# Cross-attention and an RWKV block in one kernel: the mixes behind the second norm, and the mean of the first, are emitted further behind what they read

## The chip, the cores and the metric

The kernel runs on one core of a Trainium2 chip. The metric is the device time of one execution in microseconds (us); less is better. Five engines of the core run their own instruction streams: TensorE (PE) multiplies matrices, VectorE (DVE), ScalarE (ACT) and GpSimd (POOL) do elementwise work, and SyncE (SP) issues DMA transfers. Each engine takes its instructions strictly in the order of the program; an instruction that waits for another engine holds up everything behind it on its own engine.

## The reference

`reference` chains two layers over 16 batches of 112 tokens with 512 features.

1. Cross-attention: layer norm of a context of 375 rows per batch, keys and values from it, queries from x, 16 heads of 32, softmax, output projection, and `x + tanh(gate) * out`.
2. An RWKV block: a first layer norm (`ln1`), token-shift mixes, a small tanh network that makes five mixed inputs, projections to r, k, v, gate and decay w; the recurrence

```
a = k_t[..., :, None] * v_t[..., None, :]
out = jnp.einsum('bhi,bhij->bhj', r_t, u * a + s)
s = a + w_t[..., :, None] * s
```

   over the tokens; a group norm, gate and output projection `x1 = x + og * g @ Wo.T`; a second layer norm `xc = _ln(x1, ln2_w, ln2_b)`; two mixes `xk2 = xc + sx2 * ffn_maa_k` and `xr2 = xc + sx2 * ffn_maa_r` with the token before; and `x1 + sigmoid(xr2 @ Wfr.T) * (relu(xk2 @ Wfk.T)**2 @ Wfv.T)`.

All values are float32.

## The kernel before, in words

Features lie on partitions (4 chunks of 128, called c), tokens on the free axis. Two batches make a group of N = 224 tokens; there are NG = 8 groups. Four parts are Python generators that emit instructions and yield a cost after each step:

- `attention()` runs over all 16 batches and, for each, over four sets of four heads. Names: `pa`, `pk`, `pv` (transposed context, keys L234, values L245 and their products in PSUM), `kT` (keys copied out by ScalarE, L240), `ps` (scores, L298), `pr` (scores plus mask, by VectorE, L309; exponentials in place, by ScalarE, L318), `pt`/`prT` (transposed, L329 to L338), `po`/`oR` (attention outputs and their copy by ScalarE, L353), `pp` (output projection).
- `front(g)`: first layer norm of group g (`ln1`), the difference to the token before (`sx`), the mix `mx` (L534), the tanh network (`pth`, `th`), and the five mixed inputs `xm` (`pxm`, `pxm_b`, L558, L564).
- `middle(g)`: projections `pv`, `pk`, `pr`, `pw` (L180, L684), then 16 steps n of the recurrence: keys times values `kv` (values spread over partitions by DMA, L718; products on VectorE and GpSimd, L731; the first column L739 or L741), the scan on VectorE (`st`, L754), its product with r on GpSimd (L758), and a sum on TensorE (`acc`, L770). It also emits the group norm and gate of the first half of the features (`gm`, `gv`, `gsq`).
- `back(g)`: group norm of the other half, `po1` (L180 again), the second layer norm (`ln2`, tiles `xc`, `sq2`), the two mixes `xk` and `xr` (L853 on ScalarE, L857 on VectorE), and the feed-forward products `pfk`, `pfr`, `pfv`.

The layer norm is one helper for both norms. GpSimd adds the four chunks pairwise (`halves`, L482 and L483), TensorE multiplies the sum with a constant matrix for the mean (L488), VectorE subtracts it (L496), ScalarE squares (L497) and loads its table for logarithm and exponential (L466), GpSimd adds the squares, TensorE makes the variance (L488), ScalarE makes the inverse deviation in two steps (L470, L471), and VectorE multiplies it in, in two halves (L506). For the last group's first norm and the last two groups' second norm (`late`) TensorE sums all four chunks itself. Between these steps stand the yields 2.5, 1, 4 and 1.

The order of emission is a loop at the end. Each part has a place on a common scale on which attention takes 92 cost units for one group; the part with the smallest place emits its next step, and its place grows by the step's cost times a rate. The rate of a part is its length divided by its sum of costs, `FRONT = (0.35, 38.0)`, `MIDDLE = (0.75, 119.0)`, `BACK = (0.8, 65.0)`; the last but one group has a shorter front and middle (`AHEAD_OF_LAST`). So a cost that is added in one step moves the steps behind it, against those of the other parts.

Emission is not yet the order on an engine: a scheduler of the framework places the instructions of each engine by its own estimates. What stands under `tc.high_priority(AHEAD)` goes ahead of what was emitted shortly before it; the mixes L853 and L857 and the relu L868 don't stand under it, most copies out of PSUM do.

PSUM has two pools that matter here. `ps_mm` has 2 buffers, used in turn by everything that TensorE makes for one copy (`pa`, `pk`, `pv`, `po`, `mean`, `var`, `pw`, `pfk` and so on): a tile can be begun when the copy of the tile two before it is done. `ps_s` has 4 buffers for `ps`, `pt` and `pxm`. Weights come in slabs of five buffers, and the spread `kv` has three.

## Time and profile before

| what | us |
|---|---|
| median of 3 runs | 1453.59 (1452.08 to 1453.72) |
| the profiled execution | 1452.38 |
| its span, first to last instruction | 1450.5 |
| TensorE busy in the span | 1342.6 (93%) |
| VectorE busy | 915.7 (63%) |
| ScalarE busy | 657.9 (45%) |
| GpSimd busy | 659.5 (45%) |
| mean granted TensorE clock | 0.968 |

From about 172 us to 1180 us the trace repeats itself once for each group, with a period of 166 to 170 us: the front of a group, the middle of the group before it and the back of the one before that run beside the attention of the next. The last 270 us, in which attention has ended, look different. A line of the timeline gives the start, the duration, the engine, the line of the kernel, the operation, `written<-read`, and in brackets the idle time of the engine just before it with what ended it.

### The profile page before, as it was taken

What the parts mean: (1) busy time and instruction counts of PE and PEld (TensorE: products, weight loads), DVE (VectorE), ACT (ScalarE), POOL (GpSimd) and SP (SyncE); (2) the same over time, 40 slices, a digit from 0 to 9 for tenths busy, and PEclk for the clock granted to TensorE, in tenths of its full rate; (3) what the DMA queues carried; (4) which work ended last, traced back from release to release, by engine and by line L of the source; (5) the groups of instructions that cost most, each with busy time, mean ns of one, the idle gap of its engine ahead of it and who ended that gap; (6) DMA issues with size and microseconds to landing.
All of it is one profiled execution on the core that took longest, in us unless ns stands there. A gap on an engine that the chain in (4) does not pass through costs nothing.

```text
span 1450.5 us, 23365 instructions
## 1 busy us (share of the span) xinstructions
PE 1342.6 (93%) x8516; PEld 951.4 (66%) x8516; DVE 915.7 (63%) x1750; ACT 657.9 (45%) x1527; POOL 659.5 (45%) x639
## 2 busy tenths in 40 slices
PE   6999999999999999999999999999999898788777
PEld 4557575657676676757677576866767476567546
DVE  1344647884668747765757847686567638884852
ACT  1454442564436543455525644356535345423342
POOL 2000326742656336542555426563465516664750
PEclk8999999999999999999999999999999999989979
DMA  7212024513554045431554135451545124535541
GB/s 210 78 52 68 14 90 146 161 41 102 155 162 161 30 132 165 150 103 51 175 165 149 42 102 173 143 161 30 152 155 162 46 84 133 164 112 158 168 134 56
DMA packets 116587, 171.79 MB, mean 118 GB/s; under 512 B 9770, under 2 KB 89514, under 8 KB 116346
## 3 DMA queue, kind: packets, MB, share of 16 engines
q1 hardware_dynamic: 113578, 168.11, 37.9%
q10 hardware_dynamic: 2832, 2.10, 0.5%
q8 instruction: 67, 1.10, 0.3%
q14 instruction: 46, 0.38, 0.1%
q0 software_dynamic: 64, 0.10, 0.0%
HBM read 162.95 MB, written 7.34 MB: 117 GB/s over the span
## 4 chain that ended last, share of the span: by engine, by line
PE 68%; DVE 11%; DMA 7%; ACT 5%; POOL 4%; issue 3%; SPq 2%; DVEq 0%; ACTq 0%; POOLq 0%
PE pv L245 9%; PE pk L234 9%; PE pt L329 5%; PE ps L298 5%; DMA kv<-vd 4%; PE pfv L180 3%; PE pfk L180 3%; PE pfr L180 3%; PE po L180 3%; PE acc L770 3%; DVE st L754 3%; PE pq L180 3%; PE pr L180 2%; PE pg L180 2%; PE pv L180 2%
## 5 line engine op out<-in xcount | busy, mean ns | idle before, releaser
L758 POOL TENSOR_TENSOR st<-st,r 128x448 f32<-128x448 f32 x256 | 322.0, 1272 | 208.1 <-DVE st L754 200.7
L754 DVE TENSOR_TENSOR_SCAN st<-wp,kv 128x448 f32<-128x448 f32 x256 | 267.9, 1076 | 106.5 <-ACT qT L265 33.3
L731 POOL TENSOR_TENSOR kv<-kv,k 128x444 f32<-128x444 f32 x128 | 153.4, 1201 | 95.2 <-DMA kv<-vd 94.5
L234 PE MATMUL pk<-aT,wk 128*128 128x375 f32 x512 | 182.7, 501 | 12.0 <-ACT oR L353 11.1
L245 PE MATMUL pv<-wv,aT 128*125 128x512 f32 x384 | 175.6, 601 | 1.5 <-ACT v L250 1.0
L309 DVE CUSTOM_DVE_ANT_0 pr<-ps,mb 112x375 f32<-112x375 f32 x256 | 128.0, 542 | 58.2 <-PE ps L298 58.0
L318 ACT ACTIVATE pr<-pr,mn 112x375 f32<-112x375 f32 x256 | 153.1, 601 | 4.2 <-DVE mn L309 4.1
L234 PEld LDWEIGHTS pk<-aT,wk 128*128 128x128 f32 x512 | 97.4, 198 | 70.6 <-ACT oR L353 12.8
L329 PEld LDWEIGHTS pt<-ident,pr 112*125 112x125 f32 x768 | 103.2, 190 | 36.6 <-issue 16.2
L329 PE MATMUL pt<-ident,pr 112*125 112x112 f32 x768 | 114.2, 279 | 6.1 <-DVE xm L558 5.7
L245 PEld LDWEIGHTS pv<-wv,aT 128*125 128x125 f32 x384 | 68.8, 188 | 77.8 <-issue 73.7
L731 DVE TENSOR_TENSOR kv<-kv,k 128x444 f32<-128x444 f32 x128 | 108.8, 850 | 3.3 <-DMA kv<-vd 2.1
L770 PE MATMUL acc<-st,consts 128*32 128x224 f32 x1024 | 78.3, 374 | 11.0 <-POOL st L758 9.3
L298 PE MATMUL ps<-kT,qT 32*112 32x375 f32 x512 | 84.8, 528 | 1.8 <-DVE xm L558 0.9
L466 ACT ACT_TABLE_LOAD x64 | 82.1, 1283 | 1.1
L564 POOL TENSOR_TENSOR xm<-xm,xa 128x448 f32<-128x448 f32 x48 | 59.1, 1247 | 37.9 <-DVE xm L558 37.8
L338 DVE COPY prT<-pt 125x448 f32<-125x448 f32 x80 | 49.1, 614 | 42.5 <-PE pt L329 42.5
L336 ACT COPY prT<-pt 125x448 f32<-125x448 f32 x112 | 59.1, 528 | 28.0 <-PE pt L329 27.7
L290 POOL TENSOR_SCALAR mb<-mrow 112x375 f32<-112x375 uint8 x16 | 8.9, 556 | 132.6 <-DVE mn L309 132.0
L180 PE MATMUL pfk<-xk,wfk 128*128 128x224 f32 x256 | 55.9, 372 | 10.9 <-DVE xk L857 5.6
L558 DVE SCALAR_TENSOR_TENSOR xm<-pxm,vecs,sx 128x224 f32<-128x224 f32 x128 | 47.4, 442 | 29.1 <-PE pxm L581 29.1
L240 ACT COPY kT<-pk 128x375 f32<-128x375 f32 x64 | 30.0, 469 | 72.6 <-PE pk L234 71.8
(146 smaller groups left out, 2354.0 us busy)
## 6 DMA issues: line engine op xcount, KB each, us to landing
kv<-vd SPq DMA_DIRECT2D x512, 111.5 KB
wo<-in_wo SPq DMA_DIRECT2D x32, 512.0 KB
ctx<-in_ctx SPq DMA_DIRECT2D x15, 750.0 KB
wv<-in_wv SPq DMA_DIRECT2D x16, 512.0 KB
wk<-in_wk SPq DMA_DIRECT2D x16, 512.0 KB
wr<-in_wr SPq DMA_DIRECT2D x16, 512.0 KB
wg<-in_wg SPq DMA_DIRECT2D x16, 512.0 KB
wfk<-in_wfk SPq DMA_DIRECT2D x16, 512.0 KB
```

What stands on the lines that cost most here:

```text
L180: mm_ = nc.tensor.matmul(ps[:, e * N : (e + 1) * N], w[:, k, e * P : (e + 1) * P], rhs[:, k, :], start=(k == 0), stop=(k == NC - 1),)
L234: nc.tensor.matmul(pk[:, :S], wk[:, k, m * P : (m + 1) * P], aT[:, k, :], start=(k == 0), stop=(k == NC - 1),)
L245: nc.tensor.matmul(pv[:SC, :], aT[:, k, c * SC : (c + 1) * SC], wv[:, k, :], start=(k == 0), stop=(k == NC - 1),)
L298: score = nc.tensor.matmul(ps[:T, :S], qT[r : r + HD, m, t0 : t0 + T], kT[r : r + HD, :], start=True, stop=True,)
L309: nc.vector.tensor_tensor_reduce(pr, pss[hh][:T, :S], mb, 1.0, 3.0e38, ALU.add, ALU.min, mn)
L318: exp = nc.scalar.activation(pr, pr, AF.Exp, bias=mns[b][:, h : h + 1], scale=-1.0, accum_out=dens[b][:, h : h + 1],)
L329: nc.tensor.transpose(pt[:SC, hh * T : (hh + 1) * T], prs[hh][:, c * SC : (c + 1) * SC], ident[:T, :T])
L466: nc.scalar.preload_act_table_set(table)
L731: product = engine.tensor_tensor(kv4[:, two(p), :, 1:T], kv4[:, two(p), :, 1:T], k_prev.unsqueeze(1).broadcast_to([P, 2, GB, T - 1]), ALU. ...
L754: scan = nc.vector.tensor_tensor_scan(flat(pair), w_ps[c], flat(kv[:, two(p), :]), 0.0, ALU.mult, ALU.add)
L758: nc.gpsimd.tensor_tensor(pair, pair, rs[c // 2][:, c % 2, :].unsqueeze(1).broadcast_to([P, 2, N]), ALU.mult,)
L770: part = nc.tensor.matmul(accs[c][32 * q : 32 * q + 32, :], consts[:, C_WIN + 32 * e : C_WIN + 32 * e + 32], st[:, q, :], start=(e == 0), ...
```

## The change

Two steps are moved, and two sums of costs follow.

- In `back`, a yield of 3 stands between the second norm and the mixes that read it.
- In the first norm (`front`), the step between GpSimd's sums and the mean on TensorE costs 4, not 2.5. The second norm keeps 2.5.
- `FRONT` and `BACK` have sums of 39.5 and 68 in place of 38 and 65, so that a whole part is about as long as before; every other step of these parts is then shorter on the common scale, by 3.8% and 4.4%.

No operation is added or taken away by the text of the kernel.

```diff
-FRONT, MIDDLE, BACK = (0.35, 38.0), (0.75, 119.0), (0.8, 65.0)
+FRONT, MIDDLE, BACK = (0.35, 39.5), (0.75, 119.0), (0.8, 68.0)
...
-    def layer_norm(src, dst, sq, late, name):
+    def layer_norm(src, dst, sq, late, name, adds=2.5):
...
         halves(dst, src)
-        yield 2.5
+        yield adds
         mean = mm_tile(f"{name}_mean")[:, :N]
...
-        yield from layer_norm(x, xa, wide("mx", f"sq_{g}"), g == NG - 1, f"ln1_{g}")
+        yield from layer_norm(x, xa, wide("mx", f"sq_{g}"), g == NG - 1, f"ln1_{g}", 4)
...
         yield from layer_norm(x, xc, wide("kk", f"sq2_{g}"), late, f"ln2_{g}")
 
+        yield 3
+
         mixes = []
```

## The prediction

> **What bounds the kernel now.** I read the page first (busy times), then TensorE's waits, then the timeline around the two longest kinds of wait that the change touches, then the granted clock there.

> ```profile
> span 1450.5 us, 23365 instructions
> PE 1342.6 (93%) x8516; PEld 951.4 (66%) x8516; DVE 915.7 (63%) x1750; ACT 657.9 (45%) x1527; POOL 659.5 (45%) x639
> ```

> TensorE is busy 93% of the span, so a change that moves no work can win or lose only in its idle time, 1450.5 - 1342.6 = 108 us, and in the clock. Its waits, with total, number and longest:

> ```profile
> PE pk L234 <- ACT oR L353: 11.1, 5, 2.5
> PE ln_mean L488 <- POOL xa L483: 8.1, 7, 2.3
> PE pfk L180 <- ACT v L250: 2.4, 4, 0.8
> ```

> The first comes once in each of the five periods with middle groups 1 to 5 (back groups 0 to 4). The timeline of one:

> ```profile
> 701.33 0.54 PE L488 MATMUL ln_var<-sq,consts 128*128 128x224 f32 x2
> 701.52 0.47 ACT L240 COPY kT<-pk 128x375 f32<-128x375 f32 x1 [2.00 <-PE pk L234]
> ...
> 702.28 2.07 DVE L754 TENSOR_TENSOR_SCAN st<-wp,kv 128x448 f32<-128x448 f32 x2 [2.25 <-POOL kv L739]
> ...
> 703.34 3.29 PE L180 MATMUL pk<-xm,wk 128*128 128x224 f32 x16
> ...
> 705.51 1.08 DVE L506 TENSOR_TENSOR xc<-xc,ln_r 128x448 f32<-128x448 f32 x1
> ...
> 706.64 1.04 ACT L853 ACTIVATE xk<-xc,vecs,mix_by 128x222 f32<-128x222 f32 x2 [3.77 <-DVE xc L506]
> ...
> 707.58 1.02 ACT L853 ACTIVATE xr<-xc,vecs,mix_by 128x222 f32<-128x222 f32 x2
> ...
> 708.51 0.23 ACT L353 COPY oR<-po 128x112 f32<-128x112 f32 x1
> ...
> 708.78 4.30 PE L234 MATMUL pk<-aT,wk 128*128 128x375 f32 x8 [2.15 <-ACT oR L353]
> ```

> ScalarE stands 3.77 us at the first mix, since VectorE multiplies the norm late; the copy oR behind the mixes frees the PSUM buffer of the next pk, and TensorE stands 2.15 us. VectorE is late because a scan ahead of L506 waits for GpSimd's kv (2.25 us). That pk then takes 4.30 us; in the periods at 540 and 879 us the same eight matmuls take 2.80 and 2.79. The clock there (column before the last two):

> ```profile
> 709.00:714.00 5.00, 5.00 (x15) 3.18 (x15) 5.00 (x9) 4.98 (x15) 2.25 (x2) 0.66 0.69 226
> 541.00:545.00 4.00, 3.97 (x19) 3.14 (x18) 4.00 (x7) 3.98 (x12) 2.09 (x2) 1.00 0.71 217
> ```

> So a gap of 2.2 us is followed by a slow stretch in three of the five periods (pk 4.38, 4.30, 4.47 us), which costs 1.6 us each. The second kind, the first norm's mean:

> ```profile
> 456.42 0.64 POOL L483 TENSOR_TENSOR xa<-xa 128x224 f32<-128x224 f32 x1
> 457.12 0.65 PE L488 MATMUL ln_mean<-xa,consts 128*128 128x224 f32 x2 [1.23 <-POOL xa L483]
> ...
> 458.92 0.95 ACT L497 ACTIVATE sq<-xa 128x896 f32<-128x896 f32 x1 [2.52 <-DVE xa L496]
> ...
> 462.24 0.54 PE L488 MATMUL ln_var<-sq,consts 128*128 128x224 f32 x2
> ...
> 470.95 1.54 DVE L534 SCALAR_TENSOR_TENSOR mx<-sx,vecs,xa 128x224 f32<-128x224 f32 x4
> ```

> **The change part by part.** What decides is each engine's order in the built program, before and after. The same moves recur in every period. Times below are those of the trace of before.

> *Step 1, second norm and mixes, groups 0 to 4.* On TensorE the variance moves ahead of pk (pk_10_2 beside group 2), pfk of the first half moves behind a pt and a pv. On ScalarE the order was: copy kT, Ln, Exp, two xk, two xr, oR, four exponentials, the rest. It becomes: Ln, Exp, three xk, copy kT, a kv column, one xk, three xr, oR. So kT, which was ahead of all mixes, is now behind three that wait for L506. VectorE's order becomes: first scan, one score (L309), L506 twice, second scan. Walk it: the first scan still starts at 702.28, held by kv, and takes 1.08; L309 0.54, to 703.9; the two L506 1.08 and 0.6 to 1.08, the first done at 705.0; three mixes at 0.52 end at 706.6; kT 0.47, 707.1. TensorE: pv ends at 698.96, the variance and pk follow (pk waits for the copy of v, done at 699.5) to 702.3, scores and outputs took 1.3 beyond the variance, so the next product, the receiver of kT's buffer (pk, L180), is reached at 703.6 and waits until 707.2: **3.5 us**. It ends at 710.2; oR comes at 707.1 + 0.2 + 4 x 0.52 + 0.25 = 709.6 and is no longer waited for. So the pk that started at 708.78 starts at 710.2: +1.4 us a period, +7 for five. Queued behind the mixes on ScalarE are also k's copy (713.1, needed at 713.5) and four exponentials; GpSimd's second st waits for the second scan, 1.6 us later, covered until the scan that started at 710.53. The clock: a gap of 3.5 us will be followed by the slow stretch at least as often; I take five of five, 2 x 1.6 = +3.2. Step 1: **+10.2**. Bounds: both wait and slow stretches gone, -11.1 - 3 x 1.6 = -15.9; every wait at 4.8 and all five slow, 5 x 2.5 + 3.2 = +15.7. I take the walk, since its latest link (the scan held by kv) isn't moved.

> [...]

> *Step 2, first norm, groups 1 to 5.* On TensorE the mean moves behind the four scores and an acc (0.83 + 0.40), so it is reached at 455.89 + 1.23 = 457.1, when GpSimd's sum is just done: the waits of these groups (0.4, 1.2, 2.3, 2.0, 1.4, together 7.3) go. What is late next: the squares now stand behind oR, four exponentials and a copy on ScalarE, and GpSimd's sums of them behind a kv and two st. Squares 461.75 to 462.7, sums 1.13 + 0.66, 464.5; TensorE is there at 463.5: 1.0 wait at the variance. Then the copy of kT stands ahead of the four affines (L519), which end at 470.4 instead of 468.8; sx 2.2 and mx 1.54 end at 474.2, the add for gm at 474.6, where TensorE is at 473.0: 1.6 wait. The attention value product that started at 479.17 starts at 479.7, 38.2 us after the output projection pp at 441.5. Before, these stretches took 36.66, 37.52, 39.98, 39.66 and 37.73 (starts at 274.44, 441.65, 608.03, 778.11, 945.89), the two long ones with a slow stretch. Five times 38.2 is 191.0 against 191.55: **-0.5**. Bounds: all waits and the two slow stretches gone, -7.3 - 3.2 = -10.5; both new waits unpaid by the old in all five, 5 x 2.6 - 7.3 = +5.7.

> *Step 3, pfk.* The waits for the copy of v (2.4) lose their cause, since a pt and a pv come between; the relu L868 and GpSimd's square have room (pfv starts 20 us later): **-2**, bounds -2.4 and 0.

> *Step 4, pxm_b.* po1's second half moves ahead of it (its slab was issued 50 us earlier), and one pt is put ahead of four pxm_b, the last of which waits for that pt's copy (0.53): **+1** for six groups, bounds 0 and 6 x 0.5 = +3.

> *Step 5, DMA queues.* SyncE issues the same 758 transfers; per period one wfk and one wfr slab move four or five issues back and a wq ahead, with pfk 20 us off: **0**, bounds 0 and +2 if a slab (3.6 us for wfk in the chain) is late once.

> *Step 6, the end.* For group 6 the squares and their table load move ahead of the decay exponentials wp_7_1, which the next scans need.

> ```profile
> 1340.85 0.75 ACT L706 ACTIVATE wp<-ew 128x222 f32<-128x222 f32 x2 [4.22 <-DVE wp L703]
> ...
> 1341.67 2.05 DVE L754 TENSOR_TENSOR_SCAN st<-wp,kv 128x448 f32<-128x448 f32 x2
> ```

> The squares start after the subtraction, at about 1341.3: + 0.95 + 1.28 + 0.75 = 1344.3, scans 2.6 later, and with them the buffers of the kv loads. The norm's L506 then come ahead of scans, which pays back some: **+1.5**, bounds 0 and +2.6. The scheduler also places three more table loads in the last 270 us (89 against 86), 1.283 each = 3.85; half lies beside other work: **+2**, bounds 0 and +3.9.

> Sum: 10.2 - 0.5 - 2 + 1 + 0 + 1.5 + 2 = **+12.2** on the profiled 1452.4 = 1464.6. The median of the runs stands 1.2 above that execution; I round down to **1464** for the gains that steps 2 and 3 may add.

> **The rivals.** (a) *Faster*: the wait of step 1 is short because VectorE reaches L506 earlier than I walk it. For it: mean, squares and variance all come 2 to 12 us earlier. Against: the scan ahead is held by GpSimd's kv, not by the norm. It decides if the first L506 ends before 703.5 rather than 705.0 (then the new wait is under 2); with it at 701.7 nothing is left: -15.9 - 0.5 - 2 + 1 + 3.5 = -14, 1439; halfway, 1446. (b) *Same*: slow stretches stay at three (step 1 +7), step 2 goes halfway to its bound (-5.5), step 3 -2, the end costs 0: about 0, 1453.5. (c) *Slower still*: step 1 at +15.7, step 2 +3, the end +6: +24, 1476; for it speaks that in the end VectorE and GpSimd are nearly full. (d) The change doesn't do what it says: for group 6 the mean isn't moved at all (0.6 stays), for group 7 there are no sums of GpSimd; that is small.

> **How the numbers follow.** Forecast case (1457 to 1470): 0.56. (a) 0.20, (b) 0.08, (c) 0.16. The range 1446 to 1473 leaves out the lower half of (a) and most of (c). 0.2% is 2.9 us, about what a measurement tells from no change: faster 0.20, same 0.08, slower 0.72.

> **What would show it.** Right: a line of waits "pk L180 from ACT kT L240", five times, about 3.5 each; "pk from oR" and "ln_mean from xa" gone or under 2; new waits of ln_var on sq and of gm on o near 1; more half-clock stretches after 370, 540, 710, 880 and 1045 us; xk still waiting for xc. Wrong: if kT's copy isn't waited for, step 1 falls, and with it the sign.

## The result, and the profile after

The changed kernel takes 1464.41 us (median of 8 runs, 1459.34 to 1468.18), the kernel before 1453.46 (8 runs on the same chip): ratio 1.0077, interval 1.0052 to 1.0103. The forecast was 1464.0, slower with 0.72. The total was right. Its division among the steps was not, as the experiments show: the step priced at +10.2 costs about 2 us when it is done alone, and the one priced at -0.5 costs about 9.

The profiled execution took 1468.18 us, at the upper end of the 8. Two lines of its page:

```profile
span 1466.4 us, 23399 instructions
PE 1359.1 (93%) x8516; PEld 962.3 (66%) x8516; DVE 915.7 (62%) x1750; ACT 661.2 (45%) x1530; POOL 656.5 (45%) x639
```

The span is 15.9 us longer; TensorE's busy time is 16.5 us longer, with the same 8516 matmuls. So its idle time is as it was (107.3 against 107.9 us), and the same matmuls cover more time. The list of TensorE's waits shows that one wait has taken another's place twice (total, number, longest):

```profile
PE pk L180 <- ACT kT L240: 13.4, 5, 2.7
PE ln_var L490 <- POOL sq L485: 9.1, 6, 2.7
...
PE ln_mean L490 <- POOL xa L485: 1.2, 3, 0.8
```

The wait for oR (11.1 us, five times) has become one for kT (13.4, five times), and the wait of the first norm's mean (8.1) one of its variance (9.1). The waits of pfk for v are gone. The timeline of the changed kernel at the second norm:

```profile
540.99 1.94 DVE L508 TENSOR_TENSOR xc<-xc,ln_r 128x448 f32<-128x448 f32 x2
...
542.43 1.50 ACT L857 ACTIVATE xk<-xc,vecs,mix_by 128x222 f32<-128x222 f32 x3 [4.88 <-DVE xc L508]
...
543.83 0.45 ACT L240 COPY kT<-pk 128x375 f32<-128x375 f32 x1
...
544.33 4.98 PE L180 MATMUL pk<-xm,wk 128*128 128x224 f32 x16 [2.68 <-ACT kT L240]
```

It is the order that the prediction walked: three mixes stand ahead of kT and wait for VectorE's multiplication, and the product pk waits behind kT, 2.68 us. It then takes 4.98 us for 16 matmuls that take 3.29 in the trace of before. At the first norm:

```profile
802.15 0.65 PE L490 MATMUL ln_mean<-xa,consts 128*128 128x224 f32 x2
803.37 1.14 POOL L733 TENSOR_TENSOR kv<-kv,k 128x444 f32<-128x444 f32 x1 [0.21 <-issue]
803.90 1.08 DVE L498 TENSOR_TENSOR xa<-x,ln_mean 128x896 f32<-128x896 f32 x1
806.13 2.61 POOL L760 TENSOR_TENSOR st<-st,r 128x448 f32<-128x448 f32 x2 [1.61 <-DVE st L756]
806.52 0.94 ACT L499 ACTIVATE sq<-xa 128x896 f32<-128x896 f32 x1
808.70 1.13 POOL L484 TENSOR_TENSOR sq<-sq 128x448 f32<-128x448 f32 x1
809.90 0.66 POOL L485 TENSOR_TENSOR sq<-sq 128x224 f32<-128x224 f32 x1
810.61 0.95 PE L490 MATMUL ln_var<-sq,consts 128*128 128x224 f32 x2 [1.56 <-POOL sq L485]
811.35 4.12 PE L234 MATMUL pk<-aT,wk 128*128 128x375 f32 x8
```

The mean does not wait here. But GpSimd's order now puts a product kv and two products st, which wait for VectorE's scans, ahead of the sums of squares: the squares end at 807.46, their sums begin only at 808.70 and end at 810.56, and TensorE waits 1.56 us. In the kernel before, the sums stood ahead of that kv and those st:

```profile
459.95 1.13 POOL L482 TENSOR_TENSOR sq<-sq 128x448 f32<-128x448 f32 x1 [1.79 <-ACT sq L497]
461.16 0.66 POOL L483 TENSOR_TENSOR sq<-sq 128x224 f32<-128x224 f32 x1
461.77 1.13 POOL L731 TENSOR_TENSOR kv<-kv,k 128x444 f32<-128x444 f32 x1
462.86 2.61 POOL L758 TENSOR_TENSOR st<-st,r 128x448 f32<-128x448 f32 x2
```

In the changed kernel the eight pk behind the variance take 4.12 us; in its second execution (further down), at a granted clock of 1.00, the same eight take 2.69. Behind both waits the granted clock is 0.50 (windows of the changed kernel; PE's busy time comes first behind the window's length, the granted clock stands before the last two columns):

```profile
807.40:810.80 3.40, 1.84 (x11) 1.12 (x11) 2.52 (x5) 2.34 (x5) 3.08 (x3) 1.00 0.14 53
810.80:814.20 3.40, 3.40 (x7) 2.17 (x7) 2.77 (x4) 0.84 (x2) 2.22 (x2) 0.50 0.81 289
882.50:885.90 3.40, 0.80 (x27) 0.54 (x24) 3.40 (x6) 1.83 (x5) 1.31 (x2) 1.00 0.46 112
885.90:889.30 3.40, 3.32 (x9) 3.03 (x10) 3.40 (x9) 3.40 (x12) 3.40 (x3) 0.50 0.40 124
```

Each wait is followed by 3.4 us at half clock (clock column: 0.50 in the second and the fourth line, 1.00 ahead of them). In the five periods this happens 10 times by the trace's clock record, behind all five waits at the first norm and all five for kT; the kernel before has it 5 times, behind two of the waits for the mean and three of those for oR.

To compare runs I divide each profiled span at the starts of a period: the first pk (L234) that stands more than 60 us behind the pk ahead of it. In the kernel before these are 437.9, 604.3, 774.3, 942.1 and 1109.8 us, four periods.

| profiled execution | up to the first | four periods | the rest | half-clock windows in the four |
|---|---|---|---|---|
| before | 437.9 | 672.0 | 340.6 | 4 |
| changed | 441.2 | 682.6 | 342.6 | 8 |

So 3.3 us are lost ahead of the first mark (the first of the five norms of each kind lies there), 10.6 in the four periods, 2.0 behind them.

At the end the order moved as the prediction had it (timeline of the changed kernel): squares and table load stand ahead of wp, and the scans wait 2.30 us for it.

```profile
1353.05 0.95 ACT L499 ACTIVATE sq<-xc 128x896 f32<-128x896 f32 x1 [4.63 <-DVE xc L498]
...
1354.02 1.28 ACT L466 ACT_TABLE_LOAD   x1
1355.31 0.75 ACT L708 ACTIVATE wp<-ew 128x222 f32<-128x222 f32 x2
1356.09 2.07 DVE L756 TENSOR_TENSOR_SCAN st<-wp,kv 128x448 f32<-128x448 f32 x2 [2.30 <-ACT wp L708]
```

### The profile page after: what moved, and what is told of

It is laid out like the page before. It is cut to its first block, busy times and chain, and to the rows that moved or that the text cites. A ratio compares the mean times of both kernels' runs of the same rounds, so it can differ in the third digit from the quotient of the medians.

```text
span 1466.4 us, 23399 instructions
## 1 busy us (share of the span) xinstructions
PE 1359.1 (93%) x8516; PEld 962.3 (66%) x8516; DVE 915.7 (62%) x1750; ACT 661.2 (45%) x1530; POOL 656.5 (45%) x639
## 4 chain that ended last, share of the span: by engine, by line
PE 65%; DVE 12%; DMA 6%; ACT 5%; POOL 5%; issue 4%; SPq 2%; DVEq 0%; ACTq 0%; POOLq 0%
PE pv L245 9%; PE pk L234 9%; PE pt L329 4%; PE pk L180 4%; DVE st L756 4%; PE ps L298 4%; PE pfv L180 3%; PE pfk L180 3%; DMA kv<-vd 3%; PE po L180 3%; PE pr L180 3%; PE pfr L180 3%; POOL st L760 2%; PE pq L180 2%; PE acc L772 2%
## 5 line engine op out<-in xcount | busy, mean ns | idle before, releaser
L760 POOL TENSOR_TENSOR st<-st,r 128x448 f32<-128x448 f32 x256 | 319.6, 1262 | 219.2 <-DVE st L756 218.1
L234 PE MATMUL pk<-aT,wk 128*128 128x375 f32 x512 | 182.9, 502 | 0.1
L309 DVE CUSTOM_DVE_ANT_0 pr<-ps,mb 112x375 f32<-112x375 f32 x256 | 126.9, 543 | 56.3 <-PE ps L298 56.1
L234 PEld LDWEIGHTS pk<-aT,wk 128*128 128x128 f32 x512 | 98.9, 200 | 58.9 <-issue 9.4
L733 DVE TENSOR_TENSOR kv<-kv,k 128x444 f32<-128x444 f32 x128 | 103.8, 811 | 1.6 <-DMA kv<-vd 1.6
L772 PE MATMUL acc<-st,consts 128*32 128x224 f32 x1024 | 79.0, 371 | 14.4 <-POOL st L760 7.7
L180 PE MATMUL pk<-xm,wk 128*128 128x224 f32 x256 | 60.3, 396 | 13.4 <-ACT kT L240 13.4
L180 PE MATMUL pfk<-xk,wfk 128*128 128x224 f32 x256 | 57.7, 381 | 13.6 <-DVE xk L861 6.9
L240 ACT COPY kT<-pk 128x375 f32<-128x375 f32 x64 | 30.0, 468 | 81.5 <-PE pk L234 81.0
```

Source lines behind the costliest of these rows:

```text
L180: mm_ = nc.tensor.matmul(ps[:, e * N : (e + 1) * N], w[:, k, e * P : (e + 1) * P], rhs[:, k, :], start=(k == 0), stop=(k == NC - 1),)
L234: nc.tensor.matmul(pk[:, :S], wk[:, k, m * P : (m + 1) * P], aT[:, k, :], start=(k == 0), stop=(k == NC - 1),)
L309: nc.vector.tensor_tensor_reduce(pr, pss[hh][:T, :S], mb, 1.0, 3.0e38, ALU.add, ALU.min, mn)
L733: product = engine.tensor_tensor(kv4[:, two(p), :, 1:T], kv4[:, two(p), :, 1:T], k_prev.unsqueeze(1).broadcast_to([P, 2, GB, T - 1]), ALU. ...
L760: nc.gpsimd.tensor_tensor(pair, pair, rs[c // 2][:, c % 2, :].unsqueeze(1).broadcast_to([P, 2, N]), ALU.mult,)
L772: part = nc.tensor.matmul(accs[c][32 * q : 32 * q + 32, :], consts[:, C_WIN + 32 * e : C_WIN + 32 * e + 32], st[:, q, :], start=(e == 0), ...
```

## The experiments

My theory was the prediction's: the second norm's step carries the loss, through the wait for kT and the half clock behind it. The rival: the first norm's step carries it. Diffs are against the changed kernel. All were timed against the kernel before on the same chip.

**One part of the change at a time.** First the second norm's part alone:

```diff
-FRONT, MIDDLE, BACK = (0.35, 39.5), (0.75, 119.0), (0.8, 68.0)
+FRONT, MIDDLE, BACK = (0.35, 38.0), (0.75, 119.0), (0.8, 68.0)
-    ... layer_norm(x, xa, wide("mx", f"sq_{g}"), g == NG - 1, f"ln1_{g}", 4)
+    ... layer_norm(x, xa, wide("mx", f"sq_{g}"), g == NG - 1, f"ln1_{g}")
```

> The changed kernel with the first norm as before (step of 2.5, sum 38), so only the yield of 3 behind the second norm and the sum 68. Theory (the second norm's step carries the loss, because kT's copy falls behind mixes that wait for L506): the five waits of pk L180 for ACT kT stand at 2.7 each, the five of pk for oR are gone, +6 to +11 us against the kernel before. Rival (the first norm's step carries it, by a wait at its variance and a slow stretch of the clock there): 0 to +4 us. Rival (the last 270 us carry it): +2 to +4 with a steady period as before, 168 us.

Measured: 1452.48 against 1450.75, ratio 1.0016 (0.9992 to 1.0040). My theory fell. The wait for kT is there in full, and in total next to nothing is lost:

```profile
PE pk L180 <- ACT kT L240: 13.4, 5, 2.7
...
PE ln_mean L490 <- POOL xa L485: 6.2, 7, 1.4
```

The four periods take 665.5 us, 6.5 less than before, and the rest 346.1, 5.5 more. Not all of the 6.5 is the step's: 4.8 lie at the first norm, which this run leaves as it was, and where its execution has no half-clock window and that of the kernel before has two. Between periods with the same number of such windows the step saves about 1 us (165.4 against 166.4 with none; 166.6 to 167.0 against 167.7 and 167.8 with one).

Then the first norm's part alone (the mean moved, 39.5; the second norm and 65.0 as before):

```diff
-FRONT, MIDDLE, BACK = (0.35, 39.5), (0.75, 119.0), (0.8, 68.0)
+FRONT, MIDDLE, BACK = (0.35, 39.5), (0.75, 119.0), (0.8, 65.0)
-        yield 3
```

> The changed kernel with the second norm as before (no yield of 3, sum 65), so only the first norm's step of 4 and the sum 39.5. Theory: the mean's waits go (8.1 us in all) and waits at the variance of 1.3 to 2.7 take their place, near 0, -3 to +3 us against the kernel before; pk waits for oR as before, five times 2.2 to 2.5. Rival (the first norm carries the loss): +6 to +10 us, with a slow stretch of the clock at each of the five variances.

Measured: 1460.17, ratio 1.0058 (1.0032 to 1.0083). In total the rival was right (+9.4). Its slow stretch at each of the five variances was not there: this execution has one at two of them, and behind four of the five waits for oR. Its four periods take 679.6 us, 7.6 more than before. The waits:

```profile
PE pk L234 <- ACT oR L353: 10.8, 5, 2.2
...
PE ln_var L490 <- POOL sq L485: 7.4, 6, 1.6
```

1.7 and 9.4 us over before, together 11.1: the two parts add up to the whole change's 11.0 (14.0 in its second measurement, further down).

**The last groups alone.** The change for the fronts of groups 6 and 7 and the backs of 5 to 7:

```diff
-    ... f"ln1_{g}", 4)
+    ... f"ln1_{g}", 4 if g >= NG - 2 else 2.5)
-        yield 3
+        if g >= NG - 3:
+            yield 3
+                us = {"front": 39.5 if g >= NG - 2 else 38.0, "middle": us, "back": 68.0 if g >= NG - 3 else 65.0}[name]
```

> The change for the last groups alone (front from group 6 on, back from group 5 on); the steady periods keep the steps and sums of before. Theory: the last 270 us lose 1 to 4 us (three more table loads on ScalarE, wp behind the squares) and nothing else changes: 0 to +4 us against the kernel before. Rival (the end carries the loss): +7 us or more.

Measured: 1453.26, ratio 1.0020 (0.9998 to 1.0043); the four periods are those of before (671.2), the rest is 343.5 against 340.6. The end costs about 2.5 us, within the theory's range; the interval just reaches nothing.

**The mixes behind the copy kT.** The changed kernel, with ScalarE's mixes planned behind the last copy kT:

```diff
-                nc.scalar.copy(kT[m], pk[:, :S])
+                key_copies.append(nc.scalar.copy(kT[m], pk[:, :S]))
...
+        copied = key_copies[-1]
...
+                planned_after(shifted, copied)
```

> The changed kernel, with one thing added: the mixes on ScalarE are planned behind the last copy of kT that was emitted before them (an order on the same engine, no wait). Theory: the wait of pk L180 for kT goes; oR is still behind five mixes, so the next pk waits for it about 1.3 us, which is too short for the slow stretch: 3 us less a period than the changed kernel, 15 us over five, that is 0 to -6 us against the kernel before. Rival (the position of kT is only a mark, and the late VectorE work costs the same wherever it is felt): the wait moves to oR at 2.5 or more and the time stays within 3 us of the changed kernel, +8 to +14.

Measured: 1455.87, ratio 1.0033 (1.0010 to 1.0055), between the theories: 6 to 9 us less than the changed kernel by the ratios. That a wait of 1.3 us is too short for the slow stretch was an estimate, and the traces of the two kernels show both: behind the mean's waits of 1.23 and 1.4 us in the kernel before the clock stays at 1.00, behind the variance's of 1.27 and 1.33 us in the changed kernel it is 0.50. The waits of this run:

```profile
PE pv L246 <- ACT v L251: 8.3, 6, 1.9
...
PE ln_var L491 <- POOL sq L486: 6.1, 6, 1.6
```

kT is waited for no more, and a later copy of v takes part of that back. No half-clock window is left in the four periods (667.7 us), although the wait at the variance is still there; the last section comes back to this.

**Filling the wait.** The changed kernel, TensorE repeating scores ahead of the product that waits for kT:

```diff
+            for _ in range(3 if hh and m == 2 and b % 2 and 5 <= b < 15 else 0):
+                score = nc.tensor.matmul(
+                    ps[:T, :S], qT[r : r + HD, m, t0 : t0 + T], kT[r : r + HD, :],
+                    start=True, stop=True,
+                )
```

> The changed kernel, in which TensorE repeats the scores that it has just made (three heads, three times more each, same result) just ahead of the product that waits 2.7 us for the copy kT, in the five periods: about 1.9 us of that wait is filled with work that nobody needs. Theory (the gap itself is not what costs most, the half-clock stretch after it is, 1.7 us each): the five stretches at kT go, the gap shrinks to under 1 us, the end comes no later: 8 us less than the changed kernel, +2 to +5 us against the kernel before. Rival (the clock follows something else, or the price of a stretch is hidden): within 2 us of the changed kernel, +9 to +13. If the repeats only delay what follows: above the changed kernel.

Measured: 1502.7, ratio 1.0363 (1.0331 to 1.0395). The experiment failed; it is the expectation's last case, repeats that only delay what follows. They took 4.6 us more and not 1.9 (the score group's 24 records 5.41 us against 0.82 for 6), and what comes behind them met a new wait:

```profile
PE pr L180 <- ACT k L663: 21.9, 5, 4.4
```

It says nothing on the price of the clock, which I did not get to vary by itself.

**The variance a step later too.** A whole pk between the squares and the variance:

```diff
-FRONT, MIDDLE, BACK = (0.35, 39.5), (0.75, 119.0), (0.8, 68.0)
+FRONT, MIDDLE, BACK = (0.35, 40.5), (0.75, 119.0), (0.8, 68.0)
-        yield 4
+        yield squares
-    ... f"ln1_{g}", 4)
+    ... f"ln1_{g}", 4, 5)
```

> The changed kernel, with the first norm's variance also a step further behind its squares (5 in place of 4; the front's length raised alike, 40.5), so that a whole pk (2.5 us) stands ahead of it and the four scores behind it are one group again. Theory (the first norm costs through the new wait at the variance, 1.6 us, the half-clock stretch behind it, 1.7 us, and the split scores, 0.8 us, in each of five periods): wait 0.4, no stretch, scores whole: 10 to 16 us less than the changed kernel, -6 to +1 us against the kernel before. Rival (wait and split only, the clock stays as it was): 6 to 9 us less, +2 to +5. Rival (the mean's place itself costs): within 3 us of the changed kernel.

Measured: 1469.11, ratio 1.0143 (1.0112 to 1.0173); every theory missed, it is slower still. The wait at the variance went (0.9 us in four periods), and the same chain caught TensorE at its next link:

```profile
PE gm L627 <- DVE o L780: 16.0, 7, 3.4
```

VectorE's sum o, which gm needs, stands behind what follows from the variance. Three of the four periods again have two half-clock windows, one of them now behind gm. I take this to say that not the point of the wait costs, but that the sums of squares come late for everything behind them; the exchange on GpSimd further down tests it.

**The second norm mended.** Its part alone (first norm as before), with the mixes planned behind the copies kT and oR; then the same for groups 0 to 3 only:

```diff
-                nc.scalar.copy(kT[m], pk[:, :S])
+                out_copies.append(nc.scalar.copy(kT[m], pk[:, :S]))
...
-            return nc.scalar.copy(oR[:, m, :], po[:, :T])
+            out_copies.append(nc.scalar.copy(oR[:, m, :], po[:, :T]))
...
+        copied = out_copies[-2:]
...
+                for copy in copied:
+                    planned_after(shifted, copy)
```

```diff
-        yield 3
+        if g < NG - 3:
+            yield 3
+                us = 65.0 if name == "back" and g >= NG - 3 else us
```

> The second norm's part of the change alone (the first norm as before), with ScalarE's mixes planned behind the copies kT and oR. That part alone measured +0.2%, with a 2.7 us wait for kT and a half-clock stretch in each of five periods. Theory (these two are all that keeps it from gaining): wait and stretch go, 3.5 to 4.4 us a period, of which a later copy of v takes about 1.4 back: 10 to 15 us less than the kernel before. Rival (the mixes are now late for the next product, as they were for the other order): -4 to +2 us.

> The same, for groups 0 to 3 alone; the last three groups' second norm as before. In the trace of the second norm's part alone the four steady periods were 6.4 us shorter than before and the stretch after them 5.4 us longer. Theory (the last groups lose what the steady ones gain): 3 to 5 us less than the run before this one, 13 to 19 us less than the kernel before. Rival (the end's loss is only the steady part's gain that was not needed): the same time as the run before this one.

Measured: 1445.3, ratio 0.9953 (0.9925 to 0.9981), and 1433.76, ratio 0.9898 (0.9871 to 0.9925), against 1449.12. The first gains 3.8 us by the medians and 6.8 by the ratio: not the theory's 10 to 15, and by the medians inside the rival's range (up to 4 less). Its premise was off too: the second norm's part alone has the half-clock stretch in four of five periods, not in each. The second gains 15.4, in its range, but by 11.5 us more than the first, where 3 to 5 were expected: the last groups cost more than the theory had it (6.9 us of the 11.5 show in the traces, below). The second one's waits:

```profile
PE pr L180 <- ACT k L660: 6.2, 5, 1.2
PE ln_mean L492 <- POOL xa L487: 5.9, 7, 1.3
```

Neither kT nor oR is waited for, the copy of k takes 1.2 us a period back, and no half-clock window is left in the four periods: 656.5 us, 15.5 under before. The rest takes 340.5 us there, as before, and 347.4 with the last groups moved. This version beats both kernels, by 1.0 and about 1.8 per cent.

**GpSimd's place of the sums.** In the changed kernel, the two products st of one scan are planned behind the sums of squares, in five groups. No other engine's order changes:

```diff
+                if t is sq and name[:4] == "ln1_":
+                    square_sums.append(summed)
...
+                if n == 14 and len(square_sums) == g + 2:
+                    planned_after(product, square_sums[-1])
```

> The changed kernel, with one exchange on GpSimd alone in five groups: the first norm's two sums of squares stand ahead of two products st (L760) that wait for VectorE's scans, not behind them; every other engine's order is the same. In the changed kernel's trace the squares end at 807.46, the sums start at 808.70 and end at 810.56, and TensorE waits 1.56 for them. Theory (this place on GpSimd is what the first norm's part costs): the sums end at 809.3, the wait at the variance is 0.3 and not 1.6, the window holds too little idle time for a half-clock stretch, the norm's multiplication and with it the copy of kT and the affines come 1.3 to 2.8 us earlier: 8 to 14 us less than the changed kernel, -3 to +3 us against the kernel before. Rival (as in the run with the variance moved, TensorE only meets the next link of the same chain earlier): within 4 us of the changed kernel. Rival (the st products, 1.9 us later, hold the accumulation): above the changed kernel.

> The changed kernel again, beside the others on the same chip: +9 to +13 us against the kernel before by every theory. Its trace shows whether two half-clock stretches in every period come again (theory: yes, at the variance's and at kT's wait), with the wait at the variance 1.3 to 1.6 us.

Measured: 1457.64, ratio 1.0052 (1.0026 to 1.0078), beside 1463.79, ratio 1.0092 (1.0058 to 1.0126), for the changed kernel on the same chip: 6 us less, under the 8 to 14 expected and over the rival's 4. The changed kernel's second execution missed part of its expectation: it has two half-clock windows in two of the four periods only, and its variance waits 1.55, 1.23, 1.21, 0.55 and 0.50 us in the five. The timeline with the exchange:

```profile
798.86 0.94 ACT L503 ACTIVATE sq<-xa 128x896 f32<-128x896 f32 x1
799.88 1.13 POOL L486 TENSOR_TENSOR sq<-sq 128x448 f32<-128x448 f32 x1 [2.06 <-ACT sq L503]
801.09 0.66 POOL L487 TENSOR_TENSOR sq<-sq 128x224 f32<-128x224 f32 x1
801.71 2.23 POOL L764 TENSOR_TENSOR st<-st,r 128x448 f32<-128x448 f32 x2
801.80 0.65 PE L494 MATMUL ln_var<-sq,consts 128*128 128x224 f32 x2 [0.41 <-POOL sq L487]
```

The sums start with the squares' end, the variance waits 0.41 and not 1.56 us, and no half-clock window follows the first norm in any of the five periods (from 803.7 to 807.1 us, behind this one, the granted clock is 1.00). A wait of 0.5 us at gm took part of it back. The same exchange in the first norm's part alone:

> The first norm's part of the change alone (mean behind the scores, second norm as before; it measured +0.6%), with the exchange on GpSimd of the run before (sums of squares ahead of two products st); no other engine's order differs from the first norm's part alone. In the changed kernel this exchange gave about 6 us. Theory (the place on GpSimd is most of what the first norm's part costs, by the wait at the variance and the half-clock stretches behind it): the wait at the variance falls from 1.5 to 0.4 us, the stretches at the first norm go: 5 to 9 us less than the first norm's part alone, -1 to +4 us against the kernel before. Rival (the split scores, the reordered transposes and the later copies are most of it): within 3 us of the first norm's part alone, +5 to +9.

Measured: 1451.94 against 1451.75, ratio 1.0004 (0.9983 to 1.0026), from 1.0058. As the theory said: with that one exchange on GpSimd the first norm's part costs nothing that can be measured in total. The traces say by what. Where no half clock follows, the exchange shortens the way from the first pp to the pv behind the first norm only from 38.9 us to 38.3 (in three of five periods). Over the five periods that way takes 193.1 us and not 197.9; of these 4.8 us, 3.4 are two half-clock stretches, which the part alone has at the first norm and this run has not. Nor is the part free in every place: a period without half clock takes 167.9 us with the exchange and 166.4 before, while the rest of the span is 338.3 and not 340.6. Its waits, with the remains at variance and gm:

```profile
PE gm L631 <- DVE o L786: 3.5, 7, 0.5
PE ln_var L494 <- POOL sq L487: 2.7, 6, 0.7
```

**Both mended.** The second norm as in the fastest version, the first norm's mean moved as in the change, its squares ahead of three exponentials, and the exchange on GpSimd:

```diff
+        with tc.high_priority(AHEAD if name[:4] == "ln1_" else 0):
+            with_table(nc.scalar.activation(sq, dst, AF.Square))
```

> Both parts of the change, each with its damage taken off: the second norm moved for groups 0 to 3 alone, ScalarE's mixes behind the copies kT and oR, the first norm's mean moved as in the change, its squares on ScalarE ahead of three exponentials and its sums of squares on GpSimd ahead of the st products. Theory (the first norm's mean, moved, saves its wait of 1.2 us a period once nothing else waits for it): 2 to 6 us less than the second norm's part alone so mended, which measured 1.0% under the kernel before: -17 to -21 us. Rival (the wait at the variance takes its place): -11 to -15 us.

Measured: 1439.01, ratio 0.992 (0.9893 to 0.9947): the rival's case (-10.8). The mean's place gains nothing even so. In four periods its wait fell from 5.0 to 2.3 us, and waits of 2.1 at the variance and 2.6 at gm came in.

## Why the prediction was right, and where not

**Step 1, second norm (+10.2).** The mechanism came as walked: three mixes ahead of kT, "pk L180 from ACT kT L240" five times, a half-clock stretch behind all five, oR waited for no more. The wait was 2.7 us, not 3.5: the four scores ahead of the product are split there, which the walk missed, so that TensorE arrives about 0.8 us later. The walk's +1.4 came out all the same. In the periods without half clock, the pk behind starts 14.4 us after the pv (L180) ahead of it in the second norm's part alone, and 13.0 after it before. The term that failed is the step's sum: it priced the two waits and nothing that the same move saves in the rest of the period. Two score groups that were split stand whole (0.8 us each), pfk no longer waits for v (0.7), the transposes wait 0.3 less, and a period without half clock is 165.4 us and not 166.4. Alone, the step costs 1.7 us with the end in it, and the interval reaches below nothing.

**Step 2, first norm (-0.5).** This is the step that carries the loss: +9.4 alone. It named the cause, the sums of squares behind a kv and two st on GpSimd, and mis-sized it. The wait at the variance was put at 1.0 us and is 1.3 to 2.7 (1.56, 1.27, 2.70, 1.56, 1.33). The wait of 1.6 at gm did not come, TensorE being late already. And the term that was left out is the clock: step 1 counted the half clock behind its waits, step 2 counted only that the two old stretches would go. In the profiled execution all five came (in the second one, and in the first norm's part alone, two of five). From the first pp to the pv behind the first norm, 38.2 us a period were forecast, 191.0 in all; the 191.55 that the prediction set against them count from starts 0.17 us later, and from the same starts the kernel before takes 192.4, so that the walk gives -1.4 and not -0.5. The trace has 40.62, 40.61, 41.52, 40.62 and 40.63, together 204.0 against 192.4 before: +11.6. The second execution of the changed kernel tells the shares: 38.93 where no half clock follows, 40.62 where it does, so 1.69 for each stretch, and the walk itself was 0.7 short a period.

**Steps 3 to 6.** Step 3 held: pfk's waits for v (2.4) are gone in the changed kernel and with the second norm's part alone. Step 4, +1, is of the right size: pxm_b with its gap behind takes 1.32 us and not 1.19 in the steady groups, about +0.8 for six. Step 5 held: the weights wq are waited for 4.6 us against 4.0. Step 6, +3.5, is of the right size by the run of the last groups alone (+2.5, with an interval that just reaches nothing); with the mixes behind the copies the last groups' second norm cost more, 6.9 us of the span (347.4 against 340.5).

**How the right total came about.** Over the four periods +10.6 us: a period without half clock is 168.0 us in the changed kernel (one, in its second execution) and 166.4 before (one), 4 x 1.6 = 6.4; by subtraction, the other 4.2 are left for four more half-clock windows. The two kinds of gap and the clock behind them were the right sort of cause, at the wrong norm. An overpriced step 1 and an underpriced step 2 made up for each other, to the microsecond by luck. Neither the rival "faster" nor "same" came: the first needed a new wait of under 2 us, and it was 2.7 in all five periods.

## What to carry to other kernels

When an instruction is moved, walk the queue of every engine that its successors use, and price the new gap in both currencies: the wait itself (here 2.68 us for kT and 1.56 at the variance), and the slow clock behind it where the traces show one (here 1.69 us a stretch at the first norm). A move that is written as a step of TensorE's order was decided here by two products on GpSimd, and one exchange there took back all the time that the first norm's part had cost. Test the parts of a change one at a time even when the total comes out as forecast: here two errors of 9 to 10 us cancelled, and what was useful in the change was found only by taking it apart.

## What the runs showed of the hardware

| idle time in the window | before: windows | followed by half clock | changed: windows | followed by half clock |
|---|---|---|---|---|
| under 1.0 us | 212 | 0 | 208 | 0 |
| 1.23 to 1.56 us | 4 | 0 | 3 | 3 |
| 1.99 to 2.69 us | 5 | 5 | 6 | 6 |

In the middle row stand 1.23, 1.39, 1.42 and 1.45 us for the kernel before, 1.27, 1.33 and 1.56 us (all at the variance) for the changed one. So idle time alone does not tell the two apart. What does was not shown: no run varied it.

*Waits of about one length cost 1.5 to 1.7 us of slow clock here, or none.* In the kernel before, four of the five waits for oR are of about one length. Those ahead of the pk at 708.78 and 1044.41 us (2.15 us each) fell into one window, the next window had half clock, and the pk took 4.30 and 4.47 us. Those ahead of the pk at 539.95 (2.15) and 878.56 us (2.17) fell across two windows, with 1.45 and 0.70 us idle in the two at the first and 0.78 and 1.39 at the second; the clock stayed at 1.00, and the pk took 2.80 and 2.79 us. With the mixes behind kT the variance waited 1.07, 0.74, 1.55 and 0.50 us in the four periods, and no half clock followed. By the trace the 1.55 us fell across two windows (0.67 and 0.88); in the other three periods part of the wait stood at the mean, in an earlier window (0.40, 0.74 and 1.12 us). The way from the first pp to the pv was 38.9 to 39.1 us in all four. In the second norm's part alone one of the five waits for kT, 2.67 us, fell across two windows (0.98 and 1.69), and no half clock followed it either. In the changed kernel the four periods took 682.6 us, 200 windows of 3.413, and each wait fell at about the same place of its window every time: the half-clock windows behind the variance begin at 469.5, 640.1, 810.8 and 981.5 us, those behind kT at 544.6, 715.2, 885.9 and 1056.6. In the second execution the kernel left this step. Its first two periods took 170.5 us, with two half-clock windows each, the third 168.0 with none; there the mean waits 0.94 us and the variance 0.55. The clock at the first norm, in the second period and in the third (two windows each):

```profile
632.00:635.40 3.40, 2.19 (x12) 1.47 (x12) 2.27 (x5) 2.25 (x4) 2.64 (x3) 1.00 0.16 60
635.40:638.80 3.40, 3.40 (x7) 1.76 (x6) 3.29 (x5) 0.84 (x2) 2.60 (x2) 0.50 0.91 303
802.60:806.00 3.40, 2.85 (x21) 1.89 (x14) 1.71 (x4) 2.85 (x6) 2.55 (x3) 1.00 0.11 41
806.00:809.40 3.40, 3.40 (x17) 1.59 (x16) 3.40 (x4) 1.71 (x5) 2.61 (x2) 1.00 0.77 245
```

So one program differs by up to 2.5 us a period within one execution, 10 us over four. That is about the reach of the changed kernel's runs, 1459 to 1468 us, and their granted clock goes with it: of the eight, the four at 0.958 and 0.959 took 1466 to 1468 us, the four at 0.960 to 0.964 took 1459 to 1463. The kernel before has both kinds too. Its period without half clock took 166.4 us, those with one 167.8 and 167.7, that with two 170.1.
